# Routing in pieces of two tiles, and eight unread products before the second layer

## The chip, the cores and the metric

The kernel runs on one core of a Trainium2 chip. The metric is the device time of one execution in microseconds (us), as the median over several runs. A core has five engines that run side by side and wait for each other by semaphores: TensorE (PE in the profile; its weight loads are PEld), VectorE (DVE), ScalarE (ACT), GpSimd (POOL) and SyncE (SP, which here only issues transfers). ACT and POOL issue transfers too.

## The reference

Two layers work on x, 3327 rows by 256 features. Each layer adds a graph attention and then a feed-forward to x, and each of the four parts first normalizes its input row by row (mean and variance of 256 features):

```python
x = x + _L0_gnn_ref(_layernorm(x), adj, ...)      # attention over the graph, two heads
x = x + _L0_ffn_ref(_layernorm(x)[None], ...)[0]  # 16 experts, each token goes to its best two
x = x + _L1_gnn_ref(_layernorm(x), adj, ...)      # attention over the graph, one head
x = x + _L1_ffn_ref(_layernorm(x)[None], ...)[0]  # 30 steps: tanh, silu, layernorm, 256x256 product
```

The expert part is `logits = x @ gate_w`, the two largest of 16 by softmax, and for each chosen expert `(silu(x @ w1) * (x @ w2)) @ w3`, weighted and added. The change lies in the second line (choosing the experts) and ahead of the third.

## The kernel before

**Tiles.** x is held in SBUF as 26 tiles of 128 rows (`x[:, t, :]`), one row of zeros behind the last. All arithmetic is f32.

**First attention** (`attend`, line 201). Target rows are taken in five groups, `groups0` (line 45): tiles 0 to 3, 4 to 9, 10 to 15, 16 to 21, 22 to 25. Groups are counted from 0 in the code; the text says first to fifth group. Each group has two parts, one for each head, and each part runs over 26 source tiles j. A part of six tiles makes in one step: on ACT `e` (line 252), on DVE `pT` (line 257), and on PE one product for each target tile (line 262), which adds to `acc`. `e` and `pT` have three buffers each. In the middle of a part PE and ACT prepare the factors of the next (lines 221 and 225, tile `rb`). PE takes its instructions in order, so whatever is written between two steps' products holds up the rest if it isn't ready.

**What goes beside it.** When a group's last part is done, its `closing` is a generator from which `attend` takes one piece a step (line 267): a reciprocal and an update of x for each tile (lines 235, 479), and then `route` (line 486). Work in `later` follows, one every second step, once `closing` is empty. So the routing of a group runs during the first part of the next group, and its list writes mostly during the second part.

**Routing** (`route`). It normalizes the group's tiles into `row` through `normalized` (line 123): `inverse` (line 109) takes the statistics of each tile (lines 115 and 116), a shifted variance (118), and the power -1/2 on POOL (120); then one DVE instruction a tile makes the row (127). All that is one piece. Then `row` is written to the table in DRAM (492), the rows are turned by PE (147) and copied by ACT (148), multiplied by the gate (499), and DVE finds the best two experts (514 to 530), counts (539) and computes places (546 to 552; PE 543 and 544). The pieces after that are a token list's writes, `list_tokens`: two indirect DMAs a tile, issued by POOL (565). Behind the last of them a later group's adjacency is fetched for the first two groups (`take_graph`, lines 301 and 311). Behind the third group's list writes `begin_tiles` searches for the first 16 expert tiles (`find_tiles`, lines 631 to 722): SP reads the lists back (636), PE and DVE take turns (PE 640, 649, 681, 711), and the first rows are gathered by POOL (730) and the first matrices loaded by SP (761 to 771).

**Experts** (`work_off`, line 797). 61 tiles of 128 tokens follow each other. A tile takes its rows (gathered by POOL four tiles ahead), turns them (777, 778), makes two products with `w1` and `w2` (786), `silu` and a product on ACT and DVE (816, 820), the product with `w3` (827), a weighting on DVE (830) into one of two buffers, and an indirect DMA by POOL into `given` (831). A buffer of line 830 is free once the scatter of two tiles earlier has landed. SP loads the matrices two tiles ahead (three sets). Twice in a tile one piece of `aside` is taken: the last group's closing and routing, its list writes two at a time, then `find_tiles` for all further tiles.

**Transition.** `add_results` (line 904) waits for all of `given`, reads it back and adds it to x (913); `project` (151) takes the second layer's statistics, turns tiles in pairs (147, 148), multiplies (162), and ACT scales the result (924), after which the second attention begins.

**Order.** The kernel is written for a layer that puts each engine's instructions in an order of its own, by priorities and estimated ends, and adds the semaphores; the order on an engine is then fixed.

Of the kernel before, what the change touches and what calls it, by code (L numbers as in the profile page):

```python
# [11 lines left out]
F32 = mybir.dt.float32  # L12
# [4 lines left out]
ALU = mybir.AluOpType  # L17
# [3 lines left out]
P = 128  # L21
# [5 lines left out]
MOST = 6  # L27
# [3 lines left out]
def gat_moe_gat_recurrent_ffn(ctx: ExitStack, tc: tile.TileContext, a: dict, out: bass.AP):  # L31
    nc = tc.nc
# [12 lines left out]
    groups0 = [range(0, 4), range(4, 10), range(10, 16), range(16, 22), range(22, 26)]  # L45
# [18 lines left out]
    small = ctx.enter_context(tc.tile_pool(name="small", bufs=4))  # L64
# [3 lines left out]
    x = state.tile([P, NT, D], F32, name="x")  # L68
# [37 lines left out]
    )  # L106
    nc.vector.tensor_scalar(real, real, 0.0, None, op0=ALU.is_gt)

    def inverse(src, scale=1.0):

        n = len(src)
        mv = small.tile([P, MOST, 2], F32, name="mv")
        for j in range(n):
            st = small.tile([P, 6], F32, name="st")
            nc.vector.bn_stats(st, src[j])
            nc.vector.bn_aggr(mv[:, j, :], st)
        ve = small.tile([P, MOST], F32, name="ve")
        nc.vector.tensor_scalar(ve[:, :n], mv[:, :n, 1], EPS, 1.0 / scale**2, op0=ALU.add, op1=ALU.mult)  # L118
        r = small.tile([P, MOST], F32, name="rstd")
        power = nc.gpsimd.tensor_tensor(r[:, :n], ve[:, :n], neg_half[:, :n], ALU.pow)  # L120
        return r, mv, power.ins

    def normalized(src, dst, scale=1.0):

        r, mv, power = inverse(src, scale)
        for j in range(len(src)):
            nc.vector.tensor_scalar(  # L127
                dst[j], src[j], mv[:, j, 0:1], r[:, j : j + 1], op0=ALU.subtract, op1=ALU.mult
            )
        return power  # L130
# [20 lines left out]
    def project(groups, wv, n_out, finish, work, ps, ps_p, aside, raw=True):  # L151

        pending = None

        def products(hT, t, r):
            for j in range(2):
                p = ps_p()  # L160
                for k in range(KD):
                    nc.tensor.matmul(  # L162
                        p[:, :n_out], lhsT=hT[:, j, k, :], rhs=wv[:, k, :], start=(k == 0), stop=(k == KD - 1)
                    )
                finish(t + j, p, *([r[:, j : j + 1]] if raw else []))

        for ts in groups:
            n = len(ts)
            tiles = [x[:, t, :] for t in ts]
            if raw:  # L170
                r, _, power = inverse(tiles)
            else:
                xn = work.tile([P, G, D], F32, name="xn")
                power = normalized(tiles, [xn[:, j, :] for j in range(n)])
            aside(ts, power)
            for j0 in range(0, n, 2):
                hT = turned(x[:, ts[j0] : ts[j0] + 2, :] if raw else xn[:, j0 : j0 + 2, :], work, ps)
                if pending:
                    products(*pending)
                pending = hT, ts[j0], r[:, j0 : j0 + 2] if raw else None  # L180
        products(*pending)
# [151 lines left out]
    ones_r = rec.tile([P, P], F32, name="ones_r")  # L333
# [24 lines left out]
    with ExitStack() as moe:  # L358
# [21 lines left out]
        ps = moe.enter_context(tc.tile_pool(name="ps0", bufs=4, space=PSUM))  # L380
# [6 lines left out]
        with ExitStack() as pre:  # L387
# [26 lines left out]
            for q, (s, h, k) in enumerate((s, h, k) for s in range(2) for h in range(H) for k in range(KD)):  # L414
                nc.tensor.matmul(
                    pv[:, q : q + 1], lhsT=(w1, w2)[s][:, h, k * P : (k + 1) * P], rhs=aT[:, s, h : h + 1],
                    start=True, stop=True,
# [7 lines left out]
            for h in range(H):  # L425
                for s, b in ((0, b1), (1, b2)):
                    nc.tensor.matmul(
                        pv[:, h : h + 1], lhsT=b[:, h : h + 1].to_broadcast([P, P]), rhs=aT[:, s, h : h + 1],
                        start=(s == 0), stop=(s == 1),
# [55 lines left out]

        def route(ts):

            n, t0 = len(ts), ts[0]
            whole = [P, n, E]
            normalized([x[:, t, :] for t in ts], [row[:, j, :] for j in range(n)])  # L490
            here = slice(t0 * P, (t0 + n) * P)
            nc.scalar.dma_start(table_x[here, :].rearrange("(t p) d -> p t d", p=P), row[:, :n, :])
            yield
# [16 lines left out]
            def gcol(name):  # L510
                return gate.tile([P, MOST], F32, name=name)
# [43 lines left out]
            d, both = gcol("d"), gcol("both")  # L555
# [58 lines left out]
        row = gate.tile([P, MOST, D], F32, name="row")  # L614
# [234 lines left out]

        later = deque()  # L850
        closing = attend(sc, wh, H, groups0, 3, add_scaled, route, (run, rows_p, ps, ps_o), later, True)
        ahead.append(gathered(3))
        weights(1)
# [16 lines left out]
        fW = rec.tile([P, KD, D], F32, name="fW")  # L870
# [21 lines left out]
    with ExitStack() as st:  # L892
        keep = st.enter_context(tc.tile_pool(name="keep2", bufs=1))

        s_wh = keep.tile([P, NT, 1, D + 3], F32, name="s_wh")
        wh = s_wh[:, :, :, 2:]
        sc = Scores(keep, 1, s_wh[:, :, 0, 0:2].rearrange("p t (s h) -> p t s h", h=1))
        nc.vector.memset(wh[:, :, :, D : D + 1], 1.0)
        work = st.enter_context(tc.tile_pool(name="work2", bufs=2))
        ps = st.enter_context(tc.tile_pool(name="ps2", bufs=2, space=PSUM))  # L900
        ps_o = st.enter_context(tc.tile_pool(name="ps2o", bufs=2, space=PSUM))
        names = cycle(("th", "z", "zT"))

        def add_results(some):
            for ts in some:
                n, two = len(ts), []
                for k in range(2):
                    here = slice(k * NP + ts[0] * P, k * NP + (ts[-1] + 1) * P)
                    two.append(steps.tile([P, G, D], F32, name=next(names))[:, :n, :])
                    nc.sync.dma_start(two[k], given[here, :].rearrange("(t p) d -> p t d", p=P))  # L910
                here = x[:, ts[0] : ts[-1] + 1, :]
                for k in range(2):
                    nc.vector.tensor_tensor(here, here, two[k], ALU.add)  # L913

        add_results(groups1[:3])
        count = 0

        def spot():
            nonlocal count
            count += 1  # L920
            return ps_o.tile([P, 512], F32, name=f"acc{count % 3}")

        def split1(t, p, r):
            nc.scalar.activation(s_wh[:, t, 0, : D + 2], p[:, : D + 2], AF.Copy, scale=r)
            for ts in groups1:
                if t == ts[-1]:
                    sc.finish(ts[0], t + 1)

        project(
            groups1, wv1, D + 2, split1, work, ps, spot,  # L930
            lambda ts, power: add_results(groups1[groups1.index(ts) + 3 :][:1]),
        )
        nc.vector.tensor_scalar(wh[:, NT - 1], wh[:, NT - 1], real[:, 0:1], None, op0=ALU.mult)

        run = st.enter_context(tc.tile_pool(name="edge2", bufs=3))
        rows_p = st.enter_context(tc.tile_pool(name="rows2", bufs=2))
        fin = st.enter_context(tc.tile_pool(name="fin2", bufs=2))

        def add_elu(t, pr, h, po, r):

            low = fin.tile([P, D], F32, name="low")
            high = fin.tile([P, D], F32, name="high")
            nc.vector.tensor_scalar(low[:pr], po, r, 0.0, op0=ALU.mult, op1=ALU.min)
            nc.vector.tensor_scalar(high[:pr], po, r, 0.0, op0=ALU.mult, op1=ALU.max)  # L944
            nc.scalar.activation(low[:pr], low[:pr], AF.Exp)
            nc.vector.scalar_tensor_tensor(high[:pr], low[:pr], -1.0, high[:pr], op0=ALU.add, op1=ALU.add)
            nc.vector.tensor_tensor(x[:pr, t, :], x[:pr, t, :], high[:pr], ALU.add)

        def begin_state(ts):
            here = slice(ts[0] * P, (ts[-1] + 1) * P)  # L950
            nc.sync.dma_start(kept[here, :].rearrange("(t p) d -> p t d", p=P), x[:, ts[0] : ts[-1] + 1, :])
            yield
            tiles = [x[:, t, :] for t in ts]
            normalized(tiles, tiles, S)

        attend(sc, wh, 1, groups2, 1, add_elu, begin_state, (run, rows_p, ps, ps_o), deque())

        pb = ps.tile([P, 512], F32, name="bank")[:, :D]  # L960
        for k in range(KD):
            nc.tensor.matmul(
                pb, lhsT=lb[:, k : k + 1].to_broadcast([P, P]), rhs=fW[:, k, :], start=(k == 0), stop=(k == KD - 1)
            )
        nc.vector.tensor_tensor(bb, pb, fb, ALU.add)
        nc.vector.tensor_scalar(bb, bb, S, None, op0=ALU.mult)
        pc = ps.tile([P, 512], F32, name="bank")[:, :D]
        for k in range(KD):
            nc.vector.tensor_scalar(wc[:, k, :], fW[:, k, :], lw[:, k : k + 1], None, op0=ALU.mult)
            nc.tensor.matmul(pc, lhsT=ones_r, rhs=wc[:, k, :], start=(k == 0), stop=(k == KD - 1))  # L970
        for k in range(KD):
            nc.vector.scalar_tensor_tensor(wc[:, k, :], pc, -1.0 / D, wc[:, k, :], op0=ALU.mult, op1=ALU.add)
            nc.vector.tensor_scalar(wc[:, k, :], wc[:, k, :], S, None, op0=ALU.mult)
# [122 lines left out]
```

The softmax here doesn't subtract the row's maximum and nothing guards it: scores larger than these inputs give would overflow.

## Time and profile before

| | |
|---|---|
| median of 3 runs | 1968.25 us (1965.48 to 1968.59) |
| the profiled execution's own time | 1964.56 us |
| its span, first to last instruction | 1962.6 us |
| PE busy | 1908.9 us, 97% |
| DVE busy | 1281.6 us, 65% |
| ACT busy | 1096.5 us, 56% |
| POOL busy | 936.5 us, 48% |
| first attention | about 51 to 394 us |
| experts | about 394 to 743 us |
| PE idle at the transition | 743.4 to 754.8 us |
| last stage (30 steps) | from about 1090 us |

In lines of groups and of the timeline the columns are: start in us (timeline only), duration, engine, line of the source, operation, what is written from what, shape, number; in brackets the engine's idle time before it and what ended that. Line numbers are those of the kernel before.

### The profile page before, as it was taken

The numbers are of one execution on the slowest core, as the hardware profiler recorded it, in microseconds if no ns is written. First come the engines' busy times: TensorE is split into PE (matmuls) and PEld (weight loads), VectorE is DVE, ScalarE is ACT, GpSimd is POOL, SyncE is SP. The second block draws the span as 40 slices with busy tenths as digits, with TensorE's granted clock in tenths as the row PEclk, the third lists the DMA queues.
The fourth block names the chain that finished last, engine by engine and source line by source line (L and its number), as shares of the span: only waits on it lengthen the run. The fifth ranks groups of instructions, "written<-read, shape, count | busy, mean of one in ns | idle before, by whom it ended". The sixth has DMA issues, their size and how long they took to land.

```text
span 1962.6 us, 33704 instructions
## 1 busy us (share of the span) xinstructions
PE 1908.9 (97%) x12032; PEld 1747.3 (89%) x12032; DVE 1281.6 (65%) x3827; ACT 1096.5 (56%) x1509; POOL 936.5 (48%) x864
## 2 busy tenths in 40 slices
PE   7999999999999997999999999999999999999998
PEld 6999999998999995888888888888888888888887
DVE  6887788832222225566767777777777777777778
ACT  2977766721111113666555666666666666666664
POOL 3020202353333322010000488878888887888886
PEclk9999999999999998999999999999999999999999
DMA  8978051099999874000000000000000000000003
GB/s 168 117 104 118 6 86 50 18 307 303 357 326 336 280 245 148 2 15 9 17 9 17 28 1 1 1 1 1 1 1 1 1 1 1 1 1 1 1 1 118
DMA packets 139756, 157.09 MB, mean 80 GB/s; under 512 B 52028, under 2 KB 99365, under 8 KB 139587
## 3 DMA queue, kind: packets, MB, share of 16 engines
q1 hardware_dynamic: 123466, 122.05, 20.1%
q0 software_dynamic: 11440, 28.09, 8.3%
q10 hardware_dynamic: 4680, 4.76, 0.7%
q8 instruction: 98, 1.61, 0.3%
q14 instruction: 72, 0.58, 0.1%
HBM read 164.58 MB, written 29.78 MB: 99 GB/s over the span
## 4 chain that ended last, share of the span: by engine, by line
PE 71%; issue 9%; POOL 5%; DVE 4%; DMA 3%; ACT 1%; SPq 0%; POOLq 0%; DVEq 0%; ACTq 0%
PE po L1024 35%; PE acc L262 24%; PE pt L1008 8%; POOL given L831 2%; DVE pT L257 2%; POOL rb L730 2%; DMA given<-wh,to 2%; PE bank L786 1%; PE bank L499 1%; DMA wh<-in_w_dram 1%; DMA lists<-pair,ati 1%; DVE x L913 1%; PE bank L221 0%; PE acc L162 0%; ACT zT L1019 0%
## 5 line engine op out<-in xcount | busy, mean ns | idle before, releaser
L1024 PE MATMUL po<-wc,zT 128*128 128x256 f32 x3120 | 700.3, 382 | 3.6 <-ACT zT L1019 3.6
L1024 PEld LDWEIGHTS po<-wc,zT 128*128 128x128 f32 x3120 | 583.0, 190 | 89.0 <-ACT zT L1019 11.2
L1000 POOL TENSOR_TENSOR th<-th,x 128x1024 f32<-128x1024 f32 (+1 forms) x210 | 460.8, 2216 | 120.7 <-ACT th L998 117.9
L252 ACT ACTIVATE e<-rb,minus,full 128x384 f32<-128x384 f32 (+3 forms) x494 | 400.5, 824 | 180.1 <-DVE pT L257 164.1
L257 DVE SCALAR_TENSOR_TENSOR pT<-e,part,adjT 128x384 f32<-128x384 f32 (+3 forms) x494 | 380.5, 774 | 137.5 <-PE acc L262 117.0
L1005 DVE BATCH_NORM_STATS2 stats<-z 128x6 f32<-128x256 f32 x780 | 275.1, 413 | 168.5 <-ACT z L1001 168.5
L1019 ACT COPY zT<-pt 128x512 f32<-128x512 f32 (+1 forms) x300 | 196.7, 721 | 294.1 <-PE pt L1008 294.1
L1030 DVE SCALAR_TENSOR_TENSOR x<-po,rr,bb 128x256 f32<-128x256 f32 x780 | 323.2, 475 | 48.7 <-PE po L1024 42.7
L262 PE MATMUL acc<-wh,pT 128*128 128x129 f32 x2704 | 310.1, 276 | 1.6 <-DVE pT L257 1.6
L262 PEld LDWEIGHTS acc<-wh,pT 128*128 128x128 f32 x2704 | 305.2, 192 | 2.0 <-DVE pT L257 2.0
L262 PE MATMUL acc<-s_wh,pT 128*128 128x257 f32 x1352 | 295.3, 380 | 0.8 <-DVE pT L257 0.7
L262 PEld LDWEIGHTS acc<-s_wh,pT 128*128 128x128 f32 x1352 | 255.9, 190 | 37.7 <-DVE pT L257 1.8
L120 POOL TENSOR_TENSOR rstd<-ve,neg_half 128x4 f32<-128x4 f32 (+3 forms) x28 | 30.4, 1086 | 415.1 <-DVE ve L118 331.5
L989 POOL TENSOR_TENSOR rr<-rr,neg_half 128x4 f32<-128x4 f32 (+1 forms) x210 | 207.2, 989 | 15.0
L1001 ACT ACTIVATE z<-th 128x1024 f32<-128x1024 f32 (+1 forms) x210 | 201.6, 1011 | 0.6 <-POOL th L1000 0.5
L998 ACT ACTIVATE th<-x 128x1024 f32<-128x1024 f32 (+1 forms) x210 | 198.4, 1002 | 0.9 <-DVE x L127 0.9
L1008 PE MATMUL pt<-ident,z 128*128 128x128 f32 x1560 | 189.1, 274 | 2.5 <-DVE high L944 2.5
L1008 PEld LDWEIGHTS pt<-ident,z 128*128 128x128 f32 x1560 | 178.6, 142 | 13.3 <-issue 2.9
L786 PEld LDWEIGHTS bank<-hT,wh 128*128 128x128 f32 x1280 | 149.1, 192 | 5.7 <-issue 3.7
L786 PE MATMUL bank<-hT,wh 128*128 128x128 f32 x1280 | 150.1, 275 | 3.4 <-DMA wh<-in_w_dram 3.4
L820 DVE TENSOR_TENSOR pT<-e,bank 128x512 f32<-128x512 f32 x61 | 41.9, 687 | 165.2 <-PE bank L786 165.1
L816 ACT ACTIVATE e<-bank 128x512 f32<-128x512 f32 x61 | 36.4, 597 | 196.7 <-PE bank L786 184.4
(189 smaller groups left out, 1333.5 us busy)
## 6 DMA issues: line engine op xcount, KB each, us to landing
wh<-in_w_dram SPq DMA_DIRECT2D x120, 512.0 KB
first_set<-in_w_dram SPq DMA_DIRECT2D x63, 512.0 KB
in_bytes<-in_adj_dram POOLq DMA_DIRECT2D x3, 2496.0 KB, 28.7
x<-in_x_dram SPq DMA_DIRECT2D x6, 512.0 KB
kept<-x SPq DMA_DIRECT2D x8, 384.0 KB
old<-kept SPq DMA_DIRECT2D x6, 512.0 KB
out_dram<-x SPq DMA_DIRECT2D x6, 512.0 KB
table_x<-row ACTq DMA_DIRECT2D x3, 768.0 KB
```

What stands on the lines that cost most here:

```text
L252: nc.scalar.activation(e[:, : n * P], rb[:, : n * P], AF.Relu, scale=sc.full[:, j, h : h + 1], bias=sc.minus[:, j, h : h + 1],)
L257: masked = nc.vector.scalar_tensor_tensor(pT[:, : n * P], e[:, : n * P], sc.part[:, j, h : h + 1], adjT[:, j // 2, ts[0] * P : (ts[-1] + 1 ...
L262: nc.tensor.matmul(po[c], lhsT=pT[:, c * P : (c + 1) * P], rhs=wh[:, j, h, :], start=(j == 0 and c % per_bank == 0), stop=(j == NT - 1), s ...
L786: nc.tensor.matmul(p[:, f, :], lhsT=w[:, k, f * P : (f + 1) * P], rhs=hT[:, k, :], start=(k == 0), stop=(k == KD - 1),)
L989: nc.gpsimd.tensor_tensor(r[:, :n], r[:, :n], neg_half[:, :n], ALU.pow)
L998: nc.scalar.activation(th[:, :n, :], hs, AF.Tanh, scale=1.0 / S)
L1000: nc.gpsimd.tensor_tensor(th[:, :n, :], th[:, :n, :], hs, ALU.add)
L1001: nc.scalar.activation(z[:, :n, :], th[:, :n, :], AF.Silu, scale=1.0 / S)
L1005: nc.vector.bn_stats(stats[:, j, :], z[:, j, :])
L1008: nc.tensor.transpose(pt[:, j, k, :], z[:, j, k * P : (k + 1) * P], ident)
L1024: nc.tensor.matmul(po[:, j, :], lhsT=zT[:, j, k, :], rhs=wc[:, k, :], start=(k == 0), stop=(k == KD - 1),)
L1030: nc.vector.scalar_tensor_tensor(x[:, ts[0] + j, :], po[:, j, :], rr[:, j : j + 1], bb, op0=ALU.mult, op1=ALU.add)
```

## The change

Routing's first piece is split. `measured` is the loop of statistics, now a generator with a pause after each tile; `inverse` takes measured statistics if it is given them, and measures at once for all its other callers. `route` takes the statistics with a pause after every two tiles, then shifted variance and power, a pause, then the rows with a pause after every two tiles, then the write to the table. For the last group, whose routing runs beside the experts, the pauses between pairs of tiles are left out; it gets one pause more than before, that behind the power. The arithmetic is the same.

After the reads of `given` for the first three groups of the second layer have been issued, PE gets eight products of `ones_r` with the 512 columns of `fW` (both loaded long before); they go to the two banks of the second layer's `ps` in turn, and nothing reads them.

```diff
-    def inverse(src, scale=1.0):
-
-        n = len(src)
-        mv = small.tile([P, MOST, 2], F32, name="mv")
-        for j in range(n):
+    def measured(src, mv):
+
+        for j in range(len(src)):
             st = small.tile([P, 6], F32, name="st")
             nc.vector.bn_stats(st, src[j])
             nc.vector.bn_aggr(mv[:, j, :], st)
+            yield
+
+    def inverse(src, scale=1.0, mv=None):
+
+        n = len(src)
+        if mv is None:
+            mv = small.tile([P, MOST, 2], F32, name="mv")
+            for _ in measured(src, mv):
+                pass
...
-            n, t0 = len(ts), ts[0]
+            n, t0, ends = len(ts), ts[0], ts is groups0[-1]
             whole = [P, n, E]
-            normalized([x[:, t, :] for t in ts], [row[:, j, :] for j in range(n)])
+            tiles = [x[:, t, :] for t in ts]
+            mv = small.tile([P, MOST, 2], F32, name="mv")
+            for j, _ in enumerate(measured(tiles, mv)):
+                if j % 2 and not ends:
+                    yield
+            r, _, _ = inverse(tiles, 1.0, mv)
+            yield
+            for j in range(n):
+                nc.vector.tensor_scalar(
+                    row[:, j, :], tiles[j], mv[:, j, 0:1], r[:, j : j + 1], op0=ALU.subtract, op1=ALU.mult
+                )
+                if j % 2 and not ends:
+                    yield
             here = slice(t0 * P, (t0 + n) * P)
             nc.scalar.dma_start(table_x[here, :].rearrange("(t p) d -> p t d", p=P), row[:, :n, :])
             yield
...
         add_results(groups1[:3])
+
+        for _ in range(8):
+            nc.tensor.matmul(
+                ps.tile([P, 512], F32, name="bank"), lhsT=ones_r, rhs=fW.rearrange("p k d -> p (k d)"),
+                start=True, stop=True,
+            )
         count = 0
```

## The prediction

> **What bounds the kernel now.** I read the busy shares first: TensorE (PE) is busy 1908.9 of 1962.6 us, so a change is worth only what it takes from, or adds to, PE's idle time or the work in front of it. Next the list of who waited for whom on PE, from 62 to 800 us; from there on the built order of the changed kernel differs nowhere on any engine.
>
> ```profile
> PE bank L147 <- DVE x L913: 11.7, 2, 11.4
> PE bank L147 <- DVE row L127: 4.9, 4, 1.3
> PE bank L786 <- DMA wh<-in_w_dram: 3.4, 2, 1.7
> PE acc L262 <- DVE pT L257: 1.9, 2, 1.4
> PE acc L162 <- ACT s_wh L924: 1.8, 3, 1.3
> PE bank L649 <- DVE cnt L647: 1.7, 1, 1.7
> ```
>
> Columns: us in all, times, longest. Only the second row is routing's normalization: four waits, one for each of the first four groups (1.08, 1.31, 1.32, 1.17 us at 110, 191, 270 and 349 us). The timeline of VectorE (DVE) shows what makes them, here the second group:
>
> ```profile
> 189.13 0.15 DVE L118 TENSOR_SCALAR ve<-mv 128x6 f32<-128x6 f32 x1
> 189.20 1.00 DVE L257 SCALAR_TENSOR_TENSOR pT<-e,part,adjT 128x768 f32<-128x768 f32 x1
> 191.46 2.03 DVE L127 TENSOR_SCALAR row<-x,mv,rstd 128x256 f32<-128x256 f32 x6 [1.25 <-POOL rstd L120]
> 193.40 1.01 DVE L257 SCALAR_TENSOR_TENSOR pT<-e,part,adjT 128x768 f32<-128x768 f32 x1
> ```
>
> From the variance (L118) to the first normalized row are 2.33 us, of which GpSimd's power (L120) is 1.98; then six rows in 2.03 us hold up the next pT. The third place is the first experts, where DVE stands behind the landing of a scatter:
>
> ```profile
> 447.63 0.48 DVE L830 TENSOR_SCALAR wh<-acc,weight 128x256 f32<-128x256 f32 x1 [7.36 <-DMA given<-wh,to]
> ...
> 448.79 0.15 DVE L647 TENSOR_TENSOR cnt<-cnt,taken 16x1 f32<-16x1 f32 x1
> ```
>
> Behind it in DVE's order stand L641 to L647, for which PE's L649 waits 1.72 us. The queue of GpSimd (POOL) tells why the scatter is late: seven list writes precede it.
>
> ```profile
> 436.06 2.57 POOL L565 DMA_INDIRECT lists<-pair,ati  x1 [0.30 <-issue]
> 438.93 1.01 POOL L831 DMA_INDIRECT given<-wh,to  x1 [0.30 <-issue]
> 440.24 2.54 POOL L565 DMA_INDIRECT lists<-pair,ati  x1 [0.30 <-issue]
> 443.09 0.99 POOL L831 DMA_INDIRECT given<-wh,to  x1 [0.30 <-DMA lists<-pair,ati]
> ```
>
> Last the transition, in stretches of 2 us (PE busy first, PEclk the third figure from the end):
>
> ```profile
> 744.00:746.00 2.00, 0.00 (x0) 0.00 (x0) 0.00 (x0) 0.00 (x0) 0.97 (x1) 1.00 0.38 127
> 746.00:748.00 2.00, 0.00 (x0) 0.00 (x0) 0.00 (x0) 0.00 (x0) 0.00 (x0) 0.53 0.05 12
> ...
> 758.00:760.00 2.00, 1.70 (x5) 0.82 (x4) 1.72 (x4) 0.48 (x1) 0.72 (x1) 0.56 1.08 358
> 760.00:762.00 2.00, 2.00 (x14) 1.77 (x14) 2.00 (x6) 1.45 (x3) 0.00 (x0) 1.00 1.09 357
> ```
>
> PE is idle from 743.40 to 754.80, its clock falls to half near 746 and is full again near 760.
>
> **The skill.** "TensorE: Matmul & The Clock Gate", Part 1: the clock is halved after an idle window of some 3.4 us and restored after a busy one, and the windows run free of the kernel. The trace agrees: about 13.7 us, four windows, from fall to rise. Its first table says that DVE's queue is strictly in order; the 7.36 us above, with ready work behind L830, agree. "DMA: Bandwidth & Descriptors", SWDGE vs HWDGE vs iDMA, gives GpSimd's DMAs one software queue beside those of SP and ACT, which each DMA engine serves in turn. The trace agrees: while SP's expert matrices keep the DMA engines 0.84 to 1.17 busy (426 to 446 us), POOL's scatters land 6.5 to 8.5 us after their issue; list writes in the quiet stretch at 300 us took 1.2 to 2.3.
>
> **The pieces, first to third group.** No arithmetic is removed: the same six statistics (0.39 us), six aggregates (0.08 apart), one L118, one power, six rows (0.33 apart). They are spread over six steps, and the built order moves what depends on them: the first transposes of the second group's rows stand behind 102 products of the part that they run beside instead of 63 (6.5 steps of 1.34 us later), so the four L147 waits should go. But the first two rows now follow L118 directly, with no pT between. Second group, by the trace's times: L118 at 191.1, rows from 193.4 (2.33 later), two rows 0.65, pT 1.0: ready at 195.05. PE needs it at 194.06, but twelve row-factor transposes (L221, 1.34 us net) now stand just there, so PE comes at 195.4: no wait. The next two pairs of rows (0.65 each, against a surplus of DVE of 0.41 a step) leave some 0.2. So 1.31 becomes 0.2, twice. The first group (2.0 us from L118 to its rows) has no transposes there: lack 0.95, then 0.2, so 1.15 for 1.08. L543's wait (0.26, twice) may grow by 0.25 each, since routing's tail now meets the next part's closing. Sum: 0.07 - 2.2 + 0.5 = **-1.6 us**; bounds -3.7 (all waits gone) and +0.5 (the L221 cover fails once).
>
> **Fourth group.** The three earlier groups' list writes come some six steps later, and with them the search for the first tiles (L640 to L722). Its 31 short DVE instructions stood mostly in the last six steps of the fourth group's second part, where DVE has 0.41 us spare a step; now they stand in the first seven of the fifth group's first part (four tiles: PE 0.89, DVE 0.66, spare 0.23), together with the fourth's closing and measuring. Working down DVE's order there: L681 waits 0.7 for L665; pT is late by 0.1, 0.4, 0.1, 0.5, 0.6, 0.6 in steps 7 to 12; the rows wait for the power again (0.9), and the pT behind four rows in one piece is 0.95 late. Sum 4.75, against 0.15 + 1.41 + 1.17 = 2.73 now: **+2.0 us**; bounds 0 and +3.5. The adjacency of the fifth group, ordered behind the second's last list write, landed at 270 us for use at 333: 8 us later stays hidden. So do the first gathers and the first matrices (needed at 394).
>
> **The last group and the experts.** It gets one more pause, half an expert step (2.8 us). In POOL's new order all eight list writes stand together, one scatter earlier than before in front of them and tile 5's behind them. Writes from 432.4 us, 1.27 apart, the last one or two held up as now (2.5): tile 5's scatter is issued at 444.4 to 446 instead of 443.1, and lands 6.5 to 7.5 after that issue ends, near 452.5. DVE's L830 of tile 7 waits for it, and L641 to L647 stand behind that. PE reaches L649 sooner after L640 than before (8 products, 1.9 us, where there were also 2 transposes and an expert's output), at 449.1; L647 is done at 453.4 to 454.8. Wait: 4.3 to 5.7, say 4.8. In exchange SP's list read (L636) stands one set of matrices later, so L786's wait of 1.71 goes: **4.8 - 1.72 - 1.71 = +1.4 us**; bounds -3.4 (the scatter lands by 447) and +4.
>
> **The eight products.** A 128x257 f32 product takes 0.437 us (295.3 us / 676), so 128x512 some 0.87 and eight 7.0 us. They stand behind the last expert product and depend on nothing late: 743.4 to 750.5, inside the 11.4 us of idle. Cost 0. They leave 4.3 us idle; and the new order puts the second pair's four transposes (x ready at 759.8) in front of the first pair's products, so PE idles again from 755.3. The clock will mostly be low at 759.9, and the three products (1.4 us) that ran in that hole at 756.6 come after it. PE then lacks 1.4 + some 1.6 (3.2 us more at half clock); its waits for L924 (0.22, 1.32, 0.23) absorb 1.8. **+1.0 us**; bounds -2 (warm, and no delay) and +3.
>
> **Sum**: -1.6 + 2.0 + 1.4 + 1.0 = +2.8. The profiled execution, 1964.56 us (span 1962.6 and 2.0 around it), would take 1967.4. The median of the runs, 1968.25, is 3.7 higher, with runs from 1965.5 to 1968.6; on it: **1971.0 us**. A measurement of this kernel tells some 0.2%, 3.9 us, from no change.
>
> **Rivals.** *The pieces do what they look like*: the four L147 waits (4.88) and the late pT of 1.41 (fourth group) go and nothing replaces them, the experts as now: 1968.25 - 6.3 = 1962.0. For it: the transposes really move 6.5 steps. Against: DVE's work in the fourth group and the power's 2.3 us. Chance 0.2. *The scatter decides*: tile 5's lands at 455.5 because set 10 of the matrices, no longer held up by the list read, loads at 443 to 450. L649 then waits 8 us (+4.5), with the other parts 1968.25 + 4.5 + 1.4 = 1974.2. It decides once the landing is later than about 453.5. For it: the 8.5 us that a scatter took at 427. Against: POOL's queue may drain sooner with one scatter ahead. Chance 0.3. *The products do not do what they say*: they end too early to keep the clock; that is already in the sum. If a slow branch starts them 4 us later, the clock is full at 754.8, and the hole before 759.9 halves it all the same: 1970.5.
>
> **Numbers.** Forecast (within 0.2%) 0.45, the faster rival 0.2, slower 0.35 (the second rival and 0.05 for a sum of the upper bounds). Bounds in all: -9 to +11; not all at once, so the range is 1963.0 to 1976.5, and the likeliest case alone 1966 to 1973.
>
> **What would show it.** Right: no L147 wait for rows at 190 and 270 us; a pT wait near 113; DVE late at 335 to 352; a wait of 4 to 6 us at L649, none at L786 near 456; PEclk low near 760. Wrong: L649 without a wait, or the late pT of the fourth group gone: then faster. A wait over 7 us there: slower.

## The result and the profile after

The changed kernel takes 1971.77 us (median of 20 runs) against 1968.49 us (20 runs of the kernel before beside it): ratio 1.0016, 95% interval 1.0010 to 1.0022, that is +3.2 us with an interval of 2.0 to 4.3. The profiled execution took 1971.55 us, with a span of 1969.8. The kernel before had been profiled in an execution of 1964.56 us, 4 us under its median, so the two traces differ by 7.2 us and not by 3.2. I read the traces for places, and the runs for amounts.

Line numbers are now those of the kernel named. In the changed kernel the rows are L505 (in `route`; before L127), pT L264, attention products L269, the turning of rows L154, expert products L805, hT copy L797, list search L660 to L668, expert output L849, scatter L850, eight products L937.

Who waited for whom on PE, 62 to 800 us (us in all, times, longest; "issue" stands for time in which the profile shows nothing that PE waited for, PEq for PE's own sequencer):

```profile
PE bank L154 <- DVE x L932: 6.5, 2, 4.4
PE bank L805 <- ACT hT L797: 5.5, 2, 5.4
PE acc L269 <- DVE pT L264: 2.5, 6, 0.9
PE bank L668 <- DVE cnt L666: 2.2, 1, 2.2
PE bank L937 <- PEq L900: 1.8, 1, 1.8
...
PE bank L154 <- DVE row L505: 0.2, 1, 0.2
```

The four waits for normalized rows (4.9 us before) are down to one of 0.2. The second row is new and large. To see the amounts I cut the trace at three records: from the first to the last product of the first attention, from there to the last product of the experts, and from there to the first product of the second attention.

| | attention 1 | experts | transition |
|---|---|---|---|
| before | 341.4 | 349.5 | 48.7 |
| after | 339.2 | 356.7 | 51.2 |
| difference | -2.2 | +7.2 | +2.5 |

These stages, here and below, are those of one profiled execution each, which lies up to 4.8 us from its kernel's median (with sixteen products). The row of the kernel before is from the earlier trace.

The second group's rows in the timeline of DVE:

```profile
190.46 0.16 DVE L125 TENSOR_SCALAR ve<-mv 128x6 f32<-128x6 f32 x1
192.16 0.74 DVE L505 TENSOR_SCALAR row<-x,mv,rstd 128x256 f32<-128x256 f32 x2 [1.54 <-POOL rstd L127]
192.81 1.01 DVE L264 SCALAR_TENSOR_TENSOR pT<-e,part,adjT 128x768 f32<-128x768 f32 x1
193.74 0.73 DVE L505 TENSOR_SCALAR row<-x,mv,rstd 128x256 f32<-128x256 f32 x2
```

From the variance to the first row are 1.70 us; two rows, one pT, two rows follow, and PE never waits for them.

The first experts, in the timelines of PE, ACT and DVE:

```profile
391.45 3.29 PE L805 MATMUL bank<-hT,first_set 128*128 128x128 f32 x28
394.58 0.60 PE L796 MATMUL acc<-ident,rb 128*128 128x128 f32 x4
400.55 1.86 PE L805 MATMUL bank<-hT,wh 128*128 128x128 f32 x7 [5.37 <-ACT hT L797]
```

```profile
400.13 0.65 ACT L797 COPY hT<-acc 128x256 f32<-128x256 f32 x2 [6.00 <-remote]
```

```profile
400.15 0.69 DVE L839 TENSOR_TENSOR pT<-e,bank 128x512 f32<-128x512 f32 x1 [5.27 <-remote]
```

PE's records of the second tile's transposes end at 395.18. ACT's copy of them, and DVE's product with PE's result from before them, both begin only at 400.1; "remote" means that the profile has no instruction to name for the release. I call this the stall. The clock agrees that PE stands there: it falls to 0.53 from 398 to 400 us, and to 0.50 after that.

The transition, in stretches of 2 us (PE busy first, PEclk third from the end):

```profile
756.00:758.00 2.00, 1.27 (x3) 0.20 (x2) 0.69 (x1) 0.00 (x0) 0.00 (x0) 1.00 0.86 288
758.00:760.00 2.00, 0.60 (x4) 0.42 (x4) 1.41 (x5) 0.00 (x0) 0.00 (x0) 0.99 0.91 278
760.00:762.00 2.00, 0.03 (x1) 0.00 (x0) 0.71 (x4) 0.58 (x1) 0.00 (x0) 0.50 1.05 333
...
766.00:768.00 2.00, 2.00 (x6) 1.52 (x6) 2.00 (x7) 0.63 (x2) 0.00 (x0) 0.50 1.10 348
```

The eight products end at 757.3, PE idles for most of the next 7 us, and the clock is half from 760 to 770, so the work that comes near 764 begins at half clock.

### The profile page after: what moved, and what is told of

It is laid out like the page before. It is cut to its first block, busy times and chain, and to the rows that moved or that the text cites. A ratio compares the mean times of both kernels' runs of the same rounds, so it can differ in the third digit from the quotient of the medians.

```text
span 1969.8 us, 33719 instructions
## 1 busy us (share of the span) xinstructions
PE 1920.4 (97%) x12048; PEld 1754.1 (89%) x12048; DVE 1279.1 (65%) x3827; ACT 1095.1 (56%) x1509; POOL 933.0 (47%) x864
## 3 DMA queue, kind: packets, MB, share of 16 engines
q8 instruction: 99, 1.62, 0.3%
## 4 chain that ended last, share of the span: by engine, by line
PE 74%; issue 9%; POOL 5%; DVE 3%; DMA 2%; ACT 1%; another core or an unknown queue 0%; SPq 0%; POOLq 0%; DVEq 0%; ACTq 0%
PE po L1049 35%; PE acc L269 25%; PE pt L1033 8%; POOL given L850 2%; DMA given<-wh,to 2%; POOL rb L749 2%; PE bank L805 2%; DVE pT L264 1%; PE acc L169 1%; PE acc L846 1%; PE bank L518 1%; PE bank L228 1%; ACT zT L1044 0%; PE bank L154 0%; POOL lists L584 0%
## 5 line engine op out<-in xcount | busy, mean ns | idle before, releaser
L264 DVE SCALAR_TENSOR_TENSOR pT<-e,part,adjT 128x384 f32<-128x384 f32 (+3 forms) x494 | 379.7, 774 | 140.6 <-PE acc L269 121.1
L269 PE MATMUL acc<-wh,pT 128*128 128x129 f32 x2704 | 312.6, 276 | 2.3 <-DVE pT L264 2.2
L269 PEld LDWEIGHTS acc<-wh,pT 128*128 128x128 f32 x2704 | 306.0, 192 | 4.2 <-DVE pT L264 4.1
L269 PE MATMUL acc<-s_wh,pT 128*128 128x257 f32 x1352 | 295.3, 380 | 0.7 <-DVE pT L264 0.7
L269 PEld LDWEIGHTS acc<-s_wh,pT 128*128 128x128 f32 x1352 | 255.9, 190 | 37.6 <-DVE pT L264 1.7
L127 POOL TENSOR_TENSOR rstd<-ve,neg_half 128x4 f32<-128x4 f32 (+3 forms) x28 | 28.5, 1018 | 401.9 <-DVE ve L125 314.1
L805 PEld LDWEIGHTS bank<-hT,wh 128*128 128x128 f32 x1280 | 151.2, 194 | 9.5 <-ACT hT L797 6.2
L805 PE MATMUL bank<-hT,wh 128*128 128x128 f32 x1280 | 152.7, 278 | 6.6 <-ACT hT L797 5.5
```

What stands on the lines that cost most here:

```text
L264: masked = nc.vector.scalar_tensor_tensor(pT[:, : n * P], e[:, : n * P], sc.part[:, j, h : h + 1], adjT[:, j // 2, ts[0] * P : (ts[-1] + 1 ...
L269: nc.tensor.matmul(po[c], lhsT=pT[:, c * P : (c + 1) * P], rhs=wh[:, j, h, :], start=(j == 0 and c % per_bank == 0), stop=(j == NT - 1), s ...
L805: nc.tensor.matmul(p[:, f, :], lhsT=w[:, k, f * P : (f + 1) * P], rhs=hT[:, k, :], start=(k == 0), stop=(k == KD - 1),)
```

## Experiments

They ran in three sets, on three chips, each with runs of the kernel before on the same chip. Those medians were 1963.38, 1969.21 and 1968.49 us, so a kernel is compared only inside its set. "Against before" is what the ratio differs from 1, times that median.

### First set: one part at a time

Four kernels make a square (pieces for groups one to four, yes or no; pause for the last group, yes or no) with the products beside it. *Pieces only* leaves the eight products out of the changed kernel:

```diff
-        for _ in range(8):
-            nc.tensor.matmul(
-                ps.tile([P, 512], F32, name="bank"), lhsT=ones_r, rhs=fW.rearrange("p k d -> p (k d)"),
-                start=True, stop=True,
-            )
```

> The changed kernel without the eight products; every other instruction stands in the changed kernel's order. Theory (the products cost about 2.5 us in the transition, the pieces with the last group's pause about 0.8): +0.3 to +1.3 us against before, and the second attention starts some 46 to 49 us after the last expert product. Rival (the products cost nothing, all of it is the pieces): +3 us or more. In its trace the 5.4 us idle at the first experts (second tile's hT copy) stands again if it belongs to the pieces, and is absent if it was one execution's accident.

1.0008 (0.9999 to 1.0016), +1.6 us: nearest to the theory, though a little above its range, and the rival's +3 is just inside the interval. The stall isn't there; attention, experts, transition are 339.1, 353.6, 48.2 us.

*Products only* adds these five lines to the kernel before.

> The kernel before with the eight products alone. Theory: +2 to +3 us against before: the products end 4 to 5 us before x is ready, the clock falls while the first projection products run, so the stretch from the last expert product to the second attention grows from 48.7 to about 51 us. Rival (the products keep the clock and the second half of the hole is covered): 0 to -2 us. Second rival (they are hidden, nothing changes): within 0.5 us.

1.0013 (1.0006 to 1.0019), +2.6 us: as the theory had it. Stages 341.4, 349.2, 51.7.

*Pieces without the pause* is pieces only, with the last group in one go:

```diff
             r, _, _ = inverse(tiles, 1.0, mv)
-            yield
+            if not ends:
+                yield
```

> Groups one to four measured and normalized two tiles at a time, the last group as before, no eight products. Theory (the last group's pause, which reorders GpSimd's list writes and SP's list read, is what costs time at the experts): the first attention ends 2.2 us sooner and nothing is lost later: -1.5 to -2.5 us against before, waits at the experts as before (1.7 three times). Rival (the experts start sooner than their matrices land, so the sooner end turns into a longer wait there): 0 to +1 us, with an idle stretch of 3 to 6 us of TensorE near 395 us.

0.9986 (0.9979 to 0.9993), -2.7 us: the theory, a little beyond its range. Stages 339.1, 348.9, 48.8: the attention's gain is kept.

*Pause only* drops the other pauses and keeps this one:

```diff
-                if j % 2 and not ends:
-                    yield
+                pass
             r, _, _ = inverse(tiles, 1.0, mv)
-            yield
+            if ends:
+                yield
...
-                if j % 2 and not ends:
-                    yield
```

> All groups in one go as before, but one pause between the last group's power and its rows; no eight products. Theory (the pause costs): +1 to +4 us, with the waits of the changed kernel near 438, 444 and 455 us and none on the matrices near 456. Rival (the pause is free): within 0.5 us of before.

1.0030 (1.0019 to 1.0041), +5.9 us: above the range. Stages 343.1, 354.3, 47.9. So on this chip the pause costs 4.7 us of the experts in one pair (353.6 against 348.9) and 4.8 in the other (354.3 against 349.5, from the earlier trace of the kernel before); by the runs it costs 4.3 and 5.9 us. The wait list from 390 to 480 us, without the pause and with it (pieces without the pause, then pieces only):

```profile
PE bank L669 <- DVE cnt L667: 1.7, 1, 1.7
PE bank L806 <- DMA wh<-in_w_dram: 1.6, 1, 1.6
```

```profile
PE bank L668 <- DVE cnt L666: 5.2, 1, 5.2
PE bank L805 <- DMA wh<-in_w_dram: 1.4, 1, 1.4
PE bank L805 <- DMA first_set<-in_w_dram: 0.3, 1, 0.3
```

The search's wait accounts for 3.4 us. The timelines of POOL and DVE of pieces only say where it comes from:

```profile
436.42 0.97 POOL L584 DMA_INDIRECT lists<-pair,ati  x1 [0.30 <-issue]
437.69 2.57 POOL L584 DMA_INDIRECT lists<-pair,ati  x1 [0.30 <-issue]
440.56 2.54 POOL L584 DMA_INDIRECT lists<-pair,ati  x1 [0.30 <-issue]
443.40 0.99 POOL L850 DMA_INDIRECT given<-wh,to  x1 [0.30 <-DMA lists<-pair,ati]
```

```profile
450.87 0.48 DVE L849 TENSOR_SCALAR wh<-acc,weight 128x256 f32<-128x256 f32 x1 [7.06 <-DMA given<-wh,to]
```

The last list writes stand together ahead of tile 5's scatter; DVE stands 7.06 us until it has landed. Part of the rest is the clock, in stretches of 2 us of the same kernel, then of pieces without the pause:

```profile
448.00:450.00 2.00, 0.00 (x0) 0.00 (x0) 0.00 (x0) 0.00 (x0) 1.22 (x2) 1.00 1.08 324
450.00:452.00 2.00, 0.00 (x0) 0.00 (x0) 1.02 (x6) 0.00 (x0) 0.36 (x1) 0.62 0.96 327
452.00:454.00 2.00, 1.77 (x11) 1.73 (x12) 1.37 (x9) 0.00 (x0) 0.62 (x1) 0.50 0.97 262
454.00:456.00 2.00, 2.00 (x12) 2.00 (x11) 0.00 (x0) 0.00 (x0) 0.00 (x0) 0.50 1.00 351
456.00:458.00 2.00, 2.00 (x9) 1.74 (x9) 0.69 (x1) 0.37 (x1) 0.00 (x0) 0.67 0.54 209
```

```profile
448.00:450.00 2.00, 2.00 (x12) 2.00 (x12) 1.68 (x10) 0.00 (x0) 0.98 (x1) 0.50 0.65 203
450.00:452.00 2.00, 2.00 (x13) 2.00 (x13) 0.04 (x1) 0.60 (x1) 0.01 (x1) 0.64 0.99 278
```

With the pause PE is back at 452.2 and runs at half clock for some 5 us more. Without it the clock is half as well, for some 3.4 us behind the wait of 1.7. Half of the difference, about 0.8 us, is what the pause loses by the clock; with the wait's 3.4 that is 4.2 of the 4.7, and the rest wasn't traced.

### Second set: the scatter's wait, and the products' number

*Pieces with a third place* gives an expert's output three places in turn, so that tile 7's output waits for tile 4's scatter and not for tile 5's:

```diff
+        third = hold.tile([P, D], F32, name="third")
...
-                    y0 = 6 * KD * HID + s % 2 * D
-                    y = sets[1][:, y0 : y0 + D]
+                    y0 = 6 * KD * HID + s % 3 * D
+                    y = sets[1][:, y0 : y0 + D] if s % 3 < 2 else third
```

> All pieces and the last group's pause, no eight products, and a third place for an expert's output, so that tile 7's output no longer waits until tile 5's scatter has landed; the order of every engine is that of the run with the pieces alone. Theory (that scatter, late behind eight list writes, is what the pause costs): the 5.2 us wait of the list search near 447 us falls below 2 us and the half-clock stretch after it goes, -2 to -4 us against before. Rival (the list read or the matrices decide there): a wait of over 4 us stays near 447 to 456 us, under another name, and the time stays at +0.5 to +1.5 us.

1.0007 (0.9999 to 1.0015), +1.4 us: the time is the rival's, the wait the theory's. It ran on a chip where PE stalled at the first experts for 5.43 us (absent in the first set). The search waited 1.58 us, but with the stall ahead of it (in the changed kernel, also with the stall, 2.2) this shows little.

*The same without the pause*:

> Pieces for the first four groups, the last group as before, no eight products, and the third place for an expert's output. Theory (the same wait, 1.7 us here, and the half clock behind it go too): -3.5 to -5 us against before. Rival (the matrices' landing takes the wait over): no better than without the third place, -2 to -3 us.

1.0012 (1.0005 to 1.0018), +2.4 us: a miss for both. PE stalled 5.50 us at the first experts and 3.35 us near 441.

*Four and sixteen products* on the kernel before (`range(4)`, `range(16)`):

> The kernel before with four of the products: TensorE's order of the first and second pair stays as before. Theory (the clock: the products move the idle stretch, and with it the half clock, onto the projection's work): the products end near 749 us, 6 us stay idle, half clock from about 752 to 759 or later, +0.5 to +2.5 us against before. Rival (the second pair's transposes ahead of the first pair's products are what costs): 0 +- 0.7 us.

0.9999 (0.9990 to 1.0008), -0.2 us: the rival, though the interval reaches into the theory's range. Stages 343.9, 353.1, 48.3.

> The kernel before with sixteen of the products, about 14 us, which last beyond the first pair's x and nearly to the second pair's; TensorE's order as with eight. Theory (the clock): it stays full throughout, the stretch from the last expert product to the second attention is 48 to 49.5 us, -0.5 to +1 us against before although twice the useless work is done. Rival (the products or the order itself cost): +3 us as with eight, or +4 to +7 since TensorE is still busy when x is ready.

1.0014 (1.0007 to 1.0020), +2.8 us: the rival. Stages 342.7, 356.4, 51.3, in an execution 4.8 us above the median. My theory, the clock, falls here. With four products the clock was half while the projection began, and the transition was as short as before; in its stretches:

```profile
762.00:764.00 2.00, 1.14 (x5) 0.77 (x5) 0.97 (x4) 0.59 (x1) 0.00 (x0) 0.50 1.02 331
764.00:766.00 2.00, 2.00 (x5) 1.63 (x6) 1.35 (x3) 0.00 (x0) 0.17 (x1) 0.50 1.08 370
```

With sixteen it was full throughout, and the transition was as long as with eight:

```profile
766.00:768.00 2.00, 2.00 (x6) 0.95 (x5) 0.98 (x1) 0.00 (x0) 0.00 (x0) 1.00 1.04 343
...
778.00:780.00 2.00, 1.05 (x5) 0.94 (x6) 2.00 (x5) 1.97 (x9) 0.00 (x0) 1.00 1.11 349
```

What eight and sixteen share, and four hasn't, is the order: with four all of the first pair's products stand ahead of the second pair's transposes (before, six of eight records). PE's timeline with eight (products only), then with none (pieces without the pause):

```profile
756.29 0.63 PE L147 MATMUL bank<-ident,x 128*128 128x128 f32 x4 [1.59 <-DVE x L913]
761.09 1.08 PE L147 MATMUL bank<-ident,x 128*128 128x128 f32 x4 [4.17 <-DVE x L913]
761.96 3.05 PE L162 MATMUL acc<-wv,hT 128*128 128x258 f32 x8
```

```profile
753.18 1.09 PE L154 MATMUL bank<-ident,x 128*128 128x128 f32 x4 [11.30 <-DVE x L933]
754.99 2.95 PE L169 MATMUL acc<-wv,hT 128*128 128x258 f32 x6 [0.72 <-ACT hT L155]
758.42 0.73 PE L154 MATMUL bank<-ident,x 128*128 128x128 f32 x4 [0.49 <-DVE x L933]
```

Without products, six of the first pair's eight records run while the second pair's x is still missing. With eight, the second pair's transposes stand ahead of all of them, and PE waits 4.17 us with that work behind it. From the second pair's transposes to the second attention are 32.2 us without products (758.4 to 790.7), 34.5 with eight (761.1 to 795.5) and 34.6 with sixteen (769.9 to 804.5). Sixteen speaks against the clock, but not for the order alone, since PE is still busy with the products when the first pair's x is ready. No run had eight products in the old order, so the order as the cause is read from these traces and wasn't isolated.

### Third set: the square of pause and third place on one chip

The two kernels without a third place are those of the first set, the two with it those of the second.

> The pieces with the last group's pause, no eight products, a second time, beside the other three of this set on one chip. Theory (the chip sets the level, the pause costs 4 us on any): +0.5 to +2 us against before. Rival (what the pieces gain is lost on a chip where TensorE stands still at the first experts): +2 to +4 us.

1.0004 (0.9995 to 1.0012), +0.8 us: inside the theory's range. Experts 358.5.

> As the one before it in this set, with the third place for an expert's output. Theory (tile 5's scatter holds up the list search): at least 2 us below pieces_only_b. Rival (the third place moves the wait to the matrices or to the list read): within 1 us of pieces_only_b.

1.0008 (0.9999 to 1.0018), +1.6 us by the ratio, though its median, 1968.40, is 0.8 below that of pieces only (1969.19): no difference that these runs resolve, which is the rival. Experts 355.7, in its fastest execution.

> The pieces for four groups and the last group in one go, no eight products, a second time. Theory (the pieces gain in the attention whatever the chip): -2 to -3.5 us against before. Rival (that gain belongs to the first chip; elsewhere the sooner start of the experts meets matrices that land no sooner): -0.5 to +1 us.

1.0012 (1.0005 to 1.0019), +2.4 us: the rival, and more. Experts 358.4. So the other theory, that the pause costs 4 us on any chip, falls too: here the kernel without it is 1.6 us slower than the one with it, in intervals that overlap.

> As no_pause_b with the third place. Theory (the search waits 1.7 us for a scatter here too): 0.5 to 2 us below no_pause_b. Rival (what the other chip showed, +2.3 us, belongs to the third place itself): 2 to 5 us above no_pause_b.

1.0003 (0.9995 to 1.0012), +0.6 us. That is 1.8 us below no_pause_b, as the theory had it, but the intervals overlap, and the theory's reason isn't there: the profile of no_pause_b shows no wait of the search at all. Experts 361.2, in its slowest execution.

On this chip all four stalled at the first experts. The waits of pieces only, 390 to 480 us, and of pieces with the third place:

```profile
PE bank L805 <- ACT hT L797: 5.3, 1, 5.3
PE bank L668 <- DVE cnt L666: 2.9, 1, 2.9
PE bank L805 <- issue: 1.3, 2, 1.0
PE acc L796 <- issue: 0.7, 1, 0.7
```

```profile
PE bank L806 <- ACT hT L798: 5.3, 1, 5.3
PE bank L806 <- DMA wh<-in_w_dram: 1.5, 1, 1.5
...
PE bank L669 <- issue: 0.4, 1, 0.4
```

The third place does what it was made for: with the same order on every engine, the search's wait falls from 2.9 to 0.4 us, so the scatter was its cause. But 12 us later PE waits 1.5 us for matrices, and the time doesn't follow.

What this set settles is that the -2.7 us of pieces without the pause belongs to the first chip, or to the state that it was in. The gain in the attention isn't what is lost elsewhere: it took 339.1 to 340.9 us in all nine profiles with pieces and 341.4 to 343.9 in all five without. The loss is in the experts.

The stall of 5.3 to 5.5 us stands in seven profiles, all of kernels with pieces: the changed kernel, two of the second set, four of the third. It is absent from the two of the first set that have the pieces, with the same instructions. But the two kernels of the second set without pieces lose 5.9 us too: 2.2 at the same hT copy and 3.7 near 441. So it comes with the chip or its state, and its form with the kernel. These nine profiles have one more thing in common: none of them records the landing of any of the 464 transfers, while the other five (the first set, and the trace of before) record 141 to 189 each. The trace of before, at 1964.56 us, is thus one of the state without the stall, and the +7.2 us of the experts compares two states. Where all four profiles are of the other state, in the second set, the experts took 356.9 and 356.2 us with pieces and 353.1 and 356.4 without.

What makes the stall isn't settled: PE's records end before it, ACT and DVE wait for PE's results beyond it, and nothing in the profile names a cause; without landings a transfer can't be ruled out. No experiment tried one, so it stays open.

## Why the prediction was right

The total was right: +2.8 us was forecast on 1968.25, and +3.2 (2.0 to 4.3) was measured. Two of the four terms were not. Of the signs that it had named, the changed kernel's profile shows all but one: the search waits 2.2 us and not 4 to 6.

**First to third group** (said -1.6, bounds -3.7 to +0.5). When the third group's routing is done (pT number 195 of 260), pT stands 2.7 us earlier in pieces only and 2.2 in the changed kernel's profile. The cover by the row-factor transposes was right. Three sizes were too cautious: the power takes 1.36 us (first group) and 1.70 (second) from variance to row where no pT stands between, not 2.0 and 2.33 as in the trace of before; so the first group waits 0.46 instead of 1.15, and the others nothing instead of 0.2. L562 (L543 before) still waits 0.2 and twice 0.27, not 0.25 more.

**Fourth group** (said +2.0, bounds 0 to +3.5). From there to the end of the attention pieces only gives back 0.4 us. The waits of PE from 330 to 353 us are 1.8 in all where I had summed 4.75 (the terms listed there make 4.85). The failing step is "working down DVE's order": I counted the search's DVE instructions that move into those steps, but not the products that the search has on PE, which move with them. They take PE's time while DVE catches up; that this is the reason is argued from their place and wasn't tested (the changed kernel):

```profile
335.01 0.84 PE L700 MATMUL bank<-bb,vec 16*128 16x16 f32 x6
...
337.91 1.48 PE L730 MATMUL bank<-va,row 104*128 104x16 f32 x12
```

**Last group and experts** (said 4.8 - 1.72 - 1.71 = +1.4, bounds -3.4 to +4). The mechanism was as described, and so was the wait: 5.15 us in pieces only and 5.41 in pause only, where 4.3 to 5.7 was said; the scatter was issued at 443.4 and tile 7's output went at 450.9. The stage nevertheless lost 4.7 us on the first chip, for two terms. The credit of 1.71 for the matrices wasn't due: that wait was one of the single execution that I had, and products only, with the old order there, shows 0.44 in its place. And the wait of 5 us on PE brought half clock behind it, some 0.8 us more than the short wait did, which I had priced at the transition and not here. On the third chip the search waits 2.9 us with the pause and not at all without it, yet the stage is the same (358.5 and 358.4). In the changed kernel's own profile the wait is 2.2, since the stall, in no term of mine, makes PE arrive late. Its 5.4 us, less the 1.7 that stood there before, and half clock over some 4 us of work behind it are about 5.9 of the +7.2, which for that reason isn't the price of the change.

**Eight products** (said +1.0, where 1.4 + 1.6 - 1.8 makes 1.2; bounds -2 to +3). Measured +2.6 in the first set, and 2.5 us of transition in the changed kernel. That they are hidden, end too early to keep the clock, and put the second pair's transposes first was right. The failing step is "its waits absorb 1.8". Of the two losses that I added up, the half clock (1.6) costs nothing that can be seen (four products), and the order (1.4) costs about 2.3: 32.2 us become 34.5. Six records of the missing pair are 1.4 us of it at full clock. The waits didn't absorb it, since one as long as the longest before (1.32) stays with eight products (products only):

```profile
778.12 2.01 PE L162 MATMUL acc<-wv,hT 128*128 128x258 f32 x8 [1.31 <-ACT hT L148]
```

DVE came later as well: in that profile it stands 1.11 us for ACT's first `part` (L195), in the changed kernel 1.71, and at the same instruction of the kernel before not at all. That `part` needs the first pair's products. Behind DVE's wait come the statistics, the power and ACT's scaling, and behind the scaling, in ACT's order, the hT copy that PE waits for.

**The rivals.** The faster one (1962.0) came true only as far as 2.2 us in the attention. "The scatter decides" didn't come: in no run was the search's wait over 5.5 us.

The sum held by luck, since errors cancelled: the attention came out 2.7 us better than the +0.4 of its two terms, the products 1.6 worse, and the experts worse by an amount that depends on the chip (an estimate: 1.5, if what the attention and the products leave of the +3.2 is theirs). Its weakest footing was the single trace of the kernel before, which lay 4 us under its median and had none of the stall.

## What to carry to other kernels

An instruction that nobody reads isn't free because it runs in an idle stretch: where a planner decides the order, look at what now stands ahead of what, since ready work queued behind one late operand cost more here than half clock did. When work moves between stages, move its part on every engine in the sum, and count a wait of several us on PE with the half clock that followed it here (5.2 us of wait, some 5 us of work at half clock). A wait of 1 or 2 us that one profile shows beside transfers in full flow is a property of that execution until a second one shows it too, and a gain of 2.7 us on one chip is that chip's until another shows it.

## What the hardware showed beyond that

**A short wait can cost its own length again.** In pause only PE waited 1.32 us at 192 us for rows, as before, and the clock fell behind it:

```profile
194.00:196.00 2.00, 2.00 (x16) 1.80 (x15) 2.00 (x5) 0.58 (x1) 0.00 (x0) 0.82 0.09 33
196.00:198.00 2.00, 2.00 (x11) 2.00 (x11) 0.67 (x1) 0.58 (x1) 0.00 (x0) 0.50 1.03 349
198.00:200.00 2.00, 2.00 (x17) 2.00 (x16) 0.68 (x1) 0.26 (x1) 0.00 (x0) 0.83 0.08 19
```

From there on pT stands 1.62 us later than in the kernel before, whose wait of 1.31 us at the same place left the clock full; four products shows the same 1.64. The Trainium skill, "TensorE: Matmul & The Clock Gate", Part 1, speaks of an idle window of about 3.4 us that runs free of the kernel; the half clock here lasts about as long, but the wait ahead of it was much shorter than a window, and there the measurement differs from the page. So a wait of this length has a price that varies from execution to execution, and removing the rows' waits seems to remove that too: the clock fell in the first attention in two of five profiles without pieces and in none of nine with them.

**Chips differ.** The same kernel before had medians of 1963.4, 1969.2 and 1968.5 us in the three sets, a spread as large as the largest difference that was tried here (pause only, +5.9), and pieces without the pause were 2.7 us faster on the first and 2.4 slower on the third. Each chip was used in one set, so the chip can't be told from the state that it was in.
